# Depthwise tap sums that grow in SBUF instead of PSUM, and dummy products at the start, in a scan-convolution kernel on one Trainium2 core

## The chip, the cores and the metric

The kernel runs on one core of one Trainium2 chip. The metric is device time in microseconds of one execution, measured on the chip. A core has five engines that run their own instruction streams and meet only through semaphores: TensorE (PE: matrix products, output into PSUM), VectorE (DVE), ScalarE (ACT), GpSimd (POOL) and SyncE (SP, which here issues the transfers). SBUF is the working memory, 128 partitions wide; PSUM has eight banks of 512 float32 per partition. Everything here is float32.

## The reference

The input x is 4 images of 128 channels, 96 x 96. It is group-normalised, read out as four sequences of 9216 positions (rows forward, rows reversed, columns forward, columns reversed), and each sequence goes through the same block; the four results are fused and added to x.

```python
t = grouped1x1(x, in_proj_w, in_proj_b, 4)      # 128 -> 512 channels
u, gate = t[:, :256], t[:, 256:]
u = depthwise_conv(silu(u), dw_w)               # 5 taps along the sequence, 256 channels
s  = ssm_in_w @ u                               # 32 channels each
a  = DMIN + (DMAX - DMIN) * sigmoid(ssm_delta_w @ u + b)
bb = tanh(ssm_b_w @ u + b); cc = tanh(ssm_c_w @ u + b)
h  = scan(h = a * h + bb * s)                   # along the sequence
u  = u + ssm_out_w @ (cc * h + d * s)
u  = grouped1x1(u * sigmoid(gate), mix_w, mix_b, 4)
y  = out_proj_w @ u                             # back to 128 channels
out = x + fuse_w @ concat(the four y) + fuse_b
```

The depthwise convolution is the part that the change touches. It has five taps w[c, 0..4] for each of 256 channels: u[c, n] = sum over k of w[c, k] * silu(u)[c, n + k - 2].

## The kernel before

The work is cut into 384 units: 8 phases (4 images, two scan orders each), 6 steps in a phase, 4 residues p of the position modulo 4 in a step, and two sequences s = 0, 1 that run in opposite directions. The two units of one (phase, step, p) form a pair: there are 192 pairs, four to a step, 48 steps. `pair` emits the first six pairs, `pair_on` the others, `tail` what is left over. The order of each engine's instructions is the order in which these functions are written out; nothing reorders them, so an instruction that waits holds back everything behind it on its engine.

In the call of `pair_on` for pair t stand, in this order:

- products of the input projection for later steps, and ACT's SiLU of them into the tile `sil` (line 527);
- the convolution of pair t. Channels 0 to 127 go through PE: products with the diagonal matrices `band` and `less` into PSUM (line 130), completed either by DVE from the tile `lone` (line 691, in two pairs of each four) or by the `less` products and an ACT copy (lines 715, 717). Channels 128 to 255 go through the taps: ACT multiplies tap 0 (line 742, `first_tap`), and DVE adds taps 1 to 4, each as (source * weight) + partial sum (line 744). The four DVE instructions of a pair cover 128 partitions x 768 elements each (two sequences of 384 positions);
- DVE: half a step's scan in two pairs of each four (line 819), and at some places the statistics of the next image (line 445);
- POOL: c * h, plus d * s, and a copy (lines 825, 826, 828), five pairs behind the scan's input; the addition of the finished outputs of an older pair to the accumulator `acc` (line 879, two for a pair); later in the pair the decay and b * s for the scan (lines 792, 793);
- PE: the final product with the folded weights `w_fin` for the pair seven back, the state's contribution (line 577), gate products (line 557), and last the state projections of pair t (line 130, operand `main`), which read the finished `u` of pair t;
- ACT: copies of `u` into PSUM as a seed (line 589), outputs out of PSUM (lines 860, 862), tanh and copies (lines 593, 599, 781 to 802);
- DVE: the gating of the pair six back, one instruction for each sequence (line 638), which PE's next final products read. Behind it ACT emits tap 0 of pair t + 1.

The partial sum of the taps, `part`, lies in PSUM banks 0 and 1 (`TAPS = 0`). The same two banks hold the seed and the state's contribution of sequence 0 (`SSM = 0`), so the two uses of them take turns. Only the last tap writes `us[i][:, :, 1, :]`, the half of the tile `u` in SBUF that holds channels 128 to 255. `new_u` takes the tile `u` of a pair from a ring of eight.

`start` holds the first microseconds: loads of the first image with statistics on DVE, three filler products of 512 columns as soon as a chunk of x is there (line 1188), five smaller ones tied to the last statistics, the chain of small products and DVE instructions that gives the normalised weights, the folded weights, and the first pair.

Of the kernel before, what the change touches and what calls it, by code (L numbers as in the profile page):

```python
# [47 lines left out]
P = 128  # L48
B, DIM, HH, WW = 4, 128, 96, 96
L = HH * WW  # L50
HID, MH, K = 256, 32, 5
# [8 lines left out]
N = LN * WW // R  # L60
# [8 lines left out]
def conv_preact_kernel(  # L69
# [9 lines left out]
    nc = tc.nc  # L79
# [39 lines left out]


    psum = ps.tile([P, 8, 512], F32, name="psum")
    SSM, TAPS, PROJ = 0, 0, (4, 5)
    FRONT = (7, 6, 2, 3)

    def bank(i):
        return psum[:, i, :]
# [7 lines left out]
    gmeans = wp.tile([P, 2, P], F32, name="gmean")  # L134
# [32 lines left out]
    def stats_of(b):  # L167
        if b not in stats:
            stats[b] = sp.tile([P, NSC, 6], F32, tag="bn", name=f"bn_{b}")
        return stats[b]  # L170
# [127 lines left out]
    def fresh(step):  # L298

        return step * UB < NU and step % NS < NS // 2  # L300
# [75 lines left out]
    def less_rows(s, p):  # L376
        low = 64 * ((less_of(p) + s + 1) % 2)
        return slice(low, low + 64)
# [8 lines left out]
    for q in range(R):  # L387
        r = slice(32 * q, 32 * q + 32)
        nc.gpsimd.tensor_copy(id32[r, :], ident[r, r])
    for s in range(2):  # L390
        for p in range(R):
            for k in range(2):
                r, to = slice(0, P), band[:, s, p]
                if k == less_of(p):
                    r, to = less_rows(s, p), less[:, p]
                m = R * k - p + R - 1
                shape = [r.stop - r.start, 4, 32]
# [242 lines left out]
    us = {}  # L640

    def columns(step, sil, k):

        if fresh(step):
            return sil[..., k : k + N]
        return sil[..., 1 - k : 1 - k + N][..., ::-1]
# [80 lines left out]
    def new_u(i):  # L727
        us[i] = wk.tile([P, 2, 2, N], F32, tag="u", bufs=LAG + 2, name=f"u_{units[i]['id']}")

    def taps(i, ks, first=None):  # L730

        un = units[i]
        step = un["step"]
        sil = sils[step][:, :, 1] if fresh(step) else sils[step][:, ::-1, 1, ::-1]
        part = psum[:, TAPS : TAPS + 2, :N]
        for k in ks:
            off, q = divmod(un["p"] + k, R)
            src = columns(step, sil[:, :, q, :], off)
            if k == 0 and first:
                first.tensor_scalar_mul(part, src, w_tap[:, 0:1])  # L740
            elif k == 0:
                nc.scalar.activation(part, src, AF.Copy, scale=w_tap[:, 0:1])  # L742
            else:
                nc.vector.scalar_tensor_tensor(  # L744
                    us[i][:, :, 1, :] if k == K - 1 else part,
                    src,
                    w_tap[:, k : k + 1],
                    part,
                    ALU.mult,
                    ALU.add,  # L750
                )
# [51 lines left out]

    def first_tap(i):
        if i < NU:
            taps(i, range(1))

    def scan(step, part):
# [104 lines left out]
    def pair(t):  # L913
        i = 2 * t
        banks = head_banks(t)
        if t == R:
            load_lone(1)
        if t:
            new_u(i)
            taps(i, range(1, K))  # L920
            single = alone(units[i]["p"])
            conv(i, banks, single)
            if single:
                add_lone(i, banks)
            else:
                conv_less(i, banks, False)
                for s in range(2):
                    nc.vector.tensor_copy(us[i][:, s, 0, :], bank(min(banks) + s)[:, :N])
            first_tap(i + 2)
            front(t + R, FRONT if banks == PROJ else (5, 4, 2, 3))  # L930
        recurrence(t)
        stats_chunks(t)
        load_chunks(t + 2)
        proj(i, banks)
        n, s = divmod(t, 2)
        if s == 0:
            early[0] = tile_of(n) if n < 2 else shared()[:, : 4 * N].rearrange(
                "p (s j n) -> p s j n", s=2, j=2
            )
        for j in range(2):  # L940
            gate(2 * n, s, j, 2 + j)
        for j in range(2):
            tanh_one(n, early[0], s, j, 2 + j)
        load_gate(2 * n + s + UB)
        if n == 2 and s:
            nc.sync.dma_start(keep(n), early[0])
        for g in {0: (0, 1), 1: (2, 3)}.get(t, ()):
            keep_silu(0, g)
        if t > 3:
            nc.sync.dma_start(keep(t - 4), tile_of(t - 4))  # L950
        if t > 0:
            s = tbs[i - 2][0:64, :]
            nc.gpsimd.tensor_scalar(s, s, d_sb[0:64, 0:1], None, ALU.mult)

    def pair_on(t):
        i, k, n, end = 2 * t, t % R, t - LAG, NU // 2
# [28 lines left out]
            reload.clear()  # L985
        if t < end - 2:
            send()
        new_u(i)
        taps(i, range(1, K))
        conv(i, banks, single)  # L990
        if single:
# [194 lines left out]
    def start():  # L1186
        def filler(n):
            nc.tensor.matmul(  # L1188
                bank(7)[:, :n], accf[:, bass.ds(10 * SC, P)], accf[:, bass.ds(10 * SC, n)],
                start=True, stop=True,  # L1190
            )

        def outer(d, i, copy):
            for j in range(2):
                nc.tensor.matmul(  # L1195
                    bank(i)[:, bass.ts(j, P)], w_out[:, bass.ts(j, P)], w_fuse[:, d, :],
                    start=True, stop=True,
                )
            copy(w_of[:, d].rearrange("p j c -> p (j c)"), bank(i)[:, : 2 * P])

        def inner(ds, i):
            for n, (d, j) in enumerate((d, j) for d in ds for j in range(2)):
                nc.tensor.matmul(
                    bank(i)[:, bass.ts(n, P)], w_mix[:, j, :], w_of[:, d, j, :],
                    start=n == 0, stop=True, skip_group_check=True,
                )
            to = w_fin[:, ds[0] : ds[-1] + 1].rearrange("p d j c -> p (d j c)")
            nc.vector.tensor_scalar_mul(to, bank(i), 0.5)

        last_stats = stats_of(b0)  # L1210
        pieces = stats_first(b0)
        for n in (512, 512, 512):
            filler(n)
        next(pieces)
        for c, n in ((NSC - 5, 192), (NSC - 4, 192), (NSC - 3, 192), (NSC - 2, 192), (NSC - 1, 256)):
            nc.tensor.matmul(
                bank(7)[:, :6], accf[:, bass.ds(10 * SC, P)], last_stats[:, c, :], start=True, stop=True
            )
            filler(n)
        next(pieces)  # L1220
        outer(0, 0, nc.scalar.copy)
        outer(1, 1, nc.scalar.copy)
        next(pieces)
        outer(2, 4, nc.scalar.copy)
        next(pieces)
        outer(3, 5, nc.vector.tensor_copy)
        filler(128)
        for _ in pieces:
            pass
        sils[0] = new_sil(0)  # L1230
        banks = ((2, 3), (6, 7), (0, 1), (4, 5)), ((2, 3), (6, 7), (4, 5), (2, 3))

        def burst(j, g):
            for s in range(2):
                in_proj(0, g, s, j, banks[j][TURN.index(g) if j else g][s])

        def silus(j, g):
            for s in range(2):
                silu(0, g, s, j, banks[j][TURN.index(g) if j else g][s])
            edges(0, g, j, nc.vector)  # L1240

        def load_rows(j, r):
            for s in range(2):
                load_front(1, s, slice(64 * s + 32 * j, 64 * s + 32 * j + 32), r)

        for g in range(R):
            burst(0, g)
        silus(0, 0)
        burst(1, TURN[0])
        silus(0, 1)  # L1250
        burst(1, TURN[1])
        silus(0, 2)
        inner((0, 1), 0)
        inner((2, 3), 1)
        for w in (w_of, w_fuse):
            for e in (2, 1):
                nc.gpsimd.tensor_add(w[:, 0:e], w[:, 0:e], w[:, e : 2 * e])
        load_rows(0, slice(0, R))
        load_rows(1, slice(TURN[0], TURN[0] + 1))
        silus(0, 3)  # L1260
        new_u(0)
        burst(1, TURN[2])
        silus(1, TURN[0])
        taps(0, (0,), nc.vector)
        burst(1, TURN[3])
        load_rows(1, slice(TURN[1], R))
        load_rows(1, slice(0, TURN[0]))
        silus(1, TURN[1])
        taps(0, (1,))
        conv(0, head_banks(0))  # L1270
        silus(1, TURN[2])
        taps(0, (2,))
        silus(1, TURN[3])
        conv_less(0, head_banks(0))
        taps(0, (3, 4))
        keep_lone(0)
        load_lone(0)
        pf = bank(3)
        terms = [(w_of[:, 0, j, :], b_mix[:, j : j + 1]) for j in range(2)] + [(w_fuse[:, 0, :], b_out)]
        for i, (lhsT, rhs) in enumerate(terms):  # L1280
            nc.tensor.matmul(pf[:, 0:1], lhsT, rhs, start=(i == 0), stop=(i == len(terms) - 1))
        nc.scalar.activation(b_fin, pf[:, 0:1], AF.Identity, bias=b_fuse)
# [94 lines left out]
```

## Time and profile before

| | |
|---|---|
| median of 3 runs | 1738.51 us (1736.99 to 1743.14) |
| span of the profiled execution, first to last instruction | 1735.2 us |
| PE busy | 1713.6 us, 22522 instructions |
| DVE busy | 1507.9 us, 1508 instructions |
| ACT busy | 1494.8 us, 2544 instructions |
| POOL busy | 1447.0 us, 1490 instructions |
| granted TensorE clock | 1.000 |

The span is the time of the profiled execution between its first and its last instruction; no other time is given for that execution. It lies 3.3 us under the median of the runs. The rows of the profile give engine, line, operation, the tile written and the tiles read (out<-in), partitions x elements, and a count. "L744 ... psum<-sil,small,psum" is a tap that reads the source in `sil`, the weight in `small` and the partial sum in PSUM. A duration is from start to end as the profiler saw it; an instruction that has been dispatched and is held up inside its engine looks longer.

### The profile page before, as it was taken

How to read it: one execution, taken by the hardware profiler on the slowest of the kernel's cores; microseconds unless marked ns; L12 is line 12 of the kernel's file. 1: busy time of each engine (PE TensorE's matmuls, PEld its weight loads, DVE VectorE, ACT ScalarE, POOL GpSimd, SP SyncE). 2: the span in 40 equal slices, each digit the busy share in tenths (PEclk: the TensorE clock that was granted, in tenths of full speed). 3: DMA queues.
4: the chain of work that ended last, by engine and by line, in shares of the span. 5: the costliest groups of instructions: out<-in, count | busy, mean ns of one | idle time of the engine just before them, and what ended most of it. 6: DMA issues, size and time to landing. Idle time of an engine off the chain costs nothing.

```text
span 1735.2 us, 54226 instructions
## 1 busy us (share of the span) xinstructions
PE 1713.6 (99%) x22522; PEld 644.7 (37%) x22522; DVE 1507.9 (87%) x1508; ACT 1494.8 (86%) x2544; POOL 1447.0 (83%) x1490
## 2 busy tenths in 40 slices
PE   7999999999999999999999999999999999999998
PEld 4333333343333433344333443334333333333333
DVE  6899998888889998888889999888888888888887
ACT  4888988889888888888988888888998889888875
POOL 3689889888789988888788988887878889887887
PEclk9999999999999999999999999999999999999999
DMA  7746865358884786337896487433887548643364
GB/s 244 235 147 218 288 202 151 124 206 280 275 287 139 262 267 194 118 126 263 260 308 226 150 300 251 144 123 132 294 294 239 179 144 304 201 137 133 147 226 166
DMA packets 154644, 363.66 MB, mean 210 GB/s; under 512 B 19104, under 2 KB 120864, under 8 KB 154400
## 3 DMA queue, kind: packets, MB, share of 16 engines
q1 hardware_dynamic: 154256, 360.16, 62.8%
q8 instruction: 178, 2.92, 0.7%
q14 instruction: 66, 0.54, 0.1%
q10 hardware_dynamic: 144, 0.04, 0.0%
HBM read 221.41 MB, written 138.53 MB: 207 GB/s over the span
## 4 chain that ended last, share of the span: by engine, by line
PE 95%; DVE 2%; ACT 1%; DMA 1%; issue 0%; SPq 0%; DVEq 0%; ACTq 0%
PE psum L130 81%; PE psum L577 8%; PE psum L557 5%; DVE psum L744 1%; PE psum L1188 0%; DMA acc<-in_xr 0%; DMA kept<-shared 0%; DVE u L638 0%; ACT psum L589 0%; ACT psum L742 0%; DVE u L744 0%; ACT sil L527 0%; SPq L335 0%; PE psum L1195 0%; DVE u L691 0%
## 5 line engine op out<-in xcount | busy, mean ns | idle before, releaser
L744 DVE SCALAR_TENSOR_TENSOR psum<-sil,small,psum 128x768 f32<-128x768 f32 x576 | 589.1, 1023 | 42.2 <-ACT psum L742 16.8
L130 PE MATMUL psum<-u,w_fin 128*32 128x384 f32 (+1 forms) x6192 | 541.3, 484 | 1.1 <-ACT ys L860 0.4
L130 PE MATMUL psum<-u,main 128*32 128x384 f32 x6144 | 535.0, 489 | 0.5 <-DVE u L691 0.4
L638 DVE SCALAR_TENSOR_TENSOR u<-gate,psum 128x768 f32<-128x768 f32 x376 | 341.7, 950 | 150.0 <-PE psum L577 50.8
L879 POOL TENSOR_TENSOR acc<-ys,acc 128x384 f32<-128x384 f32 x375 | 411.8, 1120 | 14.0 <-ACT ys L860 1.9
L825 POOL TENSOR_TENSOR t<-t,t 64x384 f32<-64x384 f32 (+1 forms) x192 | 287.2, 1496 | 70.6 <-DVE t L819 48.3
L589 ACT COPY psum<-u 128x768 f32<-128x768 f32 x384 | 301.4, 799 | 10.5 <-DVE u L638 4.3
L130 PEld LDWEIGHTS psum<-u,w_fin 128*32 128x32 f32 x6192 | 195.2, 109 | 309.6 <-issue 235.5
L130 PEld LDWEIGHTS psum<-u,main 128*32 128x32 f32 x6144 | 180.0, 109 | 324.5 <-issue 218.3
L130 PE MATMUL psum<-sil,band 128*32 128x384 f32 x3072 | 285.3, 488 | 0.0
L792 POOL TENSOR_SCALAR t<-tm 64x384 f32<-64x384 f32 x184 | 170.8, 928 | 114.4 <-ACT tm L781 102.4
L826 POOL TENSOR_TENSOR t<-t,t 64x384 f32<-64x384 f32 (+1 forms) x192 | 233.9, 1218 | 15.1
L793 POOL TENSOR_TENSOR t<-t,tm 64x384 f32<-64x384 f32 x192 | 213.8, 1113 | 30.2 <-ACT t L784 15.5
L577 PE MATMUL psum<-t,main 32*128 32x384 f32 x1536 | 228.1, 525 | 4.2 <-ACT psum L589 4.2
L742 ACT ACTIVATE psum<-sil,small 128x768 f32<-128x768 f32 x191 | 172.6, 904 | 65.2 <-DVE u L638 61.9
L744 DVE SCALAR_TENSOR_TENSOR u<-sil,small,psum 128x768 f32<-128x768 f32 x192 | 194.9, 1015 | 6.8
L527 ACT ACTIVATE sil<-psum,bnorm 128x385 f32<-128x385 f32 x384 | 191.6, 584 | 4.0 <-DMA edge<-sil 0.9
L557 PE MATMUL psum<-x_in,wn 32*128 32x384 f32 x768 | 161.7, 498 | 0.0
L862 ACT COPY ys<-psum 128x384 f32<-128x384 f32 x288 | 132.3, 478 | 33.0 <-PE psum L130 28.3
L130 PEld LDWEIGHTS psum<-sil,band 128*32 128x32 f32 x3072 | 88.8, 108 | 171.4 <-issue 63.1
L781 ACT ACTIVATE tm<-psum,small 128x384 f32<-128x384 f32 x192 | 110.9, 578 | 14.0 <-PE psum L130 2.3
L577 PEld LDWEIGHTS psum<-t,main 32*128 32x128 f32 x1536 | 93.9, 183 | 73.7 <-issue 41.0
(108 smaller groups left out, 1512.3 us busy)
## 6 DMA issues: line engine op xcount, KB each, us to landing
gate<-kept SPq DMA_DIRECT2D x114, 768.0 KB, 5.2
kept<-gate SPq DMA_DIRECT2D x74, 768.0 KB, 3.7
sil<-sil SPq DMA_DIRECT2D x64, 770.0 KB, 6.6
lone<-edge SPq DMA_DIRECT2D x40, 770.0 KB, 7.5
x_in<-in_xs SPq DMA_DIRECT2D x250, 96.2 KB, 3.3
edge<-sil SPq DMA_DIRECT2D x96, 192.5 KB, 3.6
out<-acc SPq DMA_DIRECT2D x46, 384.0 KB, 6.4
acc<-in_xr SPq DMA_DIRECT2D x39, 384.0 KB, 6.4
```

The costliest lines, as they stand in the source:

```text
L130: nc.tensor.matmul(o[r, : rhs.shape[-1]], lhsT, rhs, start=start, stop=stop, skip_group_check=True)
L527: nc.scalar.activation(sils[step][:, s, j, g, :], bank(bk)[:, : N + 1], AF.Silu, bias=bn[:, 1:2] if j else bn[:, 4 + g : 5 + g],)
L557: nc.tensor.matmul(bank(to)[:, :N], stats[un["b"]][0][r, s, :], x_in[s][r, q, off : off + N], start=True, stop=True)
L577: nc.tensor.matmul(bank(ssm(bi, s) + j)[:, :N], w_so[r, bass.ts(j, P)], z[r, :], start=(bi, s) not in seeded, stop=True, skip_group_check= ...
L589: nc.scalar.copy(psum[:, ssm(bi, s) : ssm(bi, s) + 2, :N], us[bi][:, s])
L638: nc.vector.scalar_tensor_tensor(v, g, 1.0, pz, ALU.add, ALU.mult)
L742: nc.scalar.activation(part, src, AF.Copy, scale=w_tap[:, 0:1])
L744: nc.vector.scalar_tensor_tensor(us[i][:, :, 1, :] if k == K - 1 else part, src, w_tap[:, k : k + 1], part, ALU.mult, ALU.add,)
L793: nc.gpsimd.tensor_mul(ta[0:64, p, :], tb[0:64, :], tm[0:64, :])
L825: engine.tensor_mul(ta[0:64, p, r], tb[64:P, r], ta[64:P, p, r])
L826: engine.tensor_add(tb[0:64, r], ta[0:64, p, r], tb[0:64, r])
L879: adder.tensor_add(part, y, part)
```

## The change

There are two parts.

First, the partial sum of the taps is the `u` tile itself. Tap 0 (ACT) writes `us[i][:, :, 1, :]`, and taps 1 to 4 (DVE) read and write it in place. Nothing is left of the taps in PSUM banks 0 and 1, whose other use stays. `new_u` moves into `first_tap`, one pair earlier in the text, since tap 0 now needs the tile.

Second, `start` begins with 108 dummy products of the matrix `gmeans` with itself: tiles of 128 x 128, 128 x 32, 32 x 32, 32 x 128 and 64 x 32 with 256 or 192 columns, into banks 0 to 3. Nothing reads the results.

```diff
-    SSM, TAPS, PROJ = 0, 0, (4, 5)
+    SSM, PROJ = 0, (4, 5)
...
-        part = psum[:, TAPS : TAPS + 2, :N]
+        part = us[i][:, :, 1, :]
...
                 nc.scalar.activation(part, src, AF.Copy, scale=w_tap[:, 0:1])
             else:
                 nc.vector.scalar_tensor_tensor(
-                    us[i][:, :, 1, :] if k == K - 1 else part,
+                    part,
                     src,
                     w_tap[:, k : k + 1],
                     part,
...
     def first_tap(i):
         if i < NU:
+            new_u(i)
             taps(i, range(1))
...
         if t:
-            new_u(i)
             taps(i, range(1, K))
...
-        new_u(i)
         taps(i, range(1, K))
...
+        warm = gmeans.rearrange("p e c -> p (e c)")
+
+        def tiles(rows, cols, n=2 * P):
+            for r in range(0, P, rows):
+                for c in range(0, P, cols):
+                    nc.tensor.matmul(
+                        psum[c : c + cols, r // 32, :n], warm[r : r + rows, c : c + cols],
+                        warm[r : r + rows, :n], start=True, stop=True, skip_group_check=True,
+                    )
+
+        for shape in ((128, 128),) * 4 + (
+            (128, 32), (32, 32), (32, 32, 192), (32, 32, 192), (32, 128), (32, 32), (64, 32),
+            (32, 32), (128, 32), (128, 32),
+        ):
+            tiles(*shape)
         last_stats = stats_of(b0)
```

On DVE, two consecutive pairs in the first image, before. The scan's half comes from line 819, the gating from line 638, the taps from line 744; names of `u` are phase, step, p and s.

```order
L819 SCALAR_TENSOR_TENSOR t_2_1132<-t_2_1132,t_1_769 64x768
L638 SCALAR_TENSOR_TENSOR u_1_3_0_904<-gate_176,psum 128x768 x2
L744 SCALAR_TENSOR_TENSOR psum<-sil_747,small,psum 128x2x384 x3
L744 SCALAR_TENSOR_TENSOR u_3_2_0_1521<-sil_747,small,psum 128x2x384
L819 SCALAR_TENSOR_TENSOR t_2_1132<-t_2_1132 64x768
L638 SCALAR_TENSOR_TENSOR u_1_0_0_983<-gate_177,psum 128x768 x2
```

The same place after the change (the scan is at line 820 there):

```order
L820 SCALAR_TENSOR_TENSOR t_2_1241<-t_2_1241,t_1_878 64x768
L638 SCALAR_TENSOR_TENSOR u_1_3_0_932<-gate_176,psum 128x768 x2
L744 SCALAR_TENSOR_TENSOR u_3_2_0_1596<-sil_856,small,u_3_2_0_1596 128x2x384 x4
L820 SCALAR_TENSOR_TENSOR t_2_1241<-t_2_1241 64x768
L638 SCALAR_TENSOR_TENSOR u_1_0_0_1042<-gate_177,psum 128x768 x2
```

The instructions and their order are the same; all four taps now have both tensor inputs in SBUF (`sil` and `u`), where before each had one in SBUF and one in PSUM.

On ACT, around tap 0 in the same image, before, with the semaphores that each instruction waits for:

```order
L593 ACTIVATE gate_176<-psum,bnorm_272 128x384 [waits DMAHW5_49,PE_49]
L593 ACTIVATE gate_176<-psum,bnorm_272 128x384 [waits PE_49]
L742 ACTIVATE psum<-sil_747,small 128x2x384 [waits DVE_49]
L599 ACTIVATE gate_176<-psum,bnorm_272 128x2x384
L781 ACTIVATE tm_2_2_0_1241<-psum,small 128x384 [waits PE_49,Pool_49]
```

And after:

```order
L593 ACTIVATE gate_176<-psum,bnorm_380 128x384 [waits DMAHW5_49,PE_49]
L593 ACTIVATE gate_176<-psum,bnorm_380 128x384 [waits PE_49]
L742 ACTIVATE u_2_3_0_1327<-sil_856,small 128x2x384
L599 ACTIVATE gate_176<-psum,bnorm_380 128x2x384
L781 ACTIVATE tm_2_2_0_1350<-psum,small 128x384 [waits PE_49,Pool_49]
```

Tap 0 no longer waits for DVE's gating, which read banks 0 and 1; it stands at the same place.

On PE, the head of the program before:

```order
L1372 UNCONDITIONAL_BRANCH
L1188 MATMUL psum<-acc 128x512 x3
L1216 MATMUL psum<-bn_94,acc 128x6
L1188 MATMUL psum<-acc 128x192
L1216 MATMUL psum<-bn_94,acc 128x6
```

And after:

```order
L1386 UNCONDITIONAL_BRANCH
L1214 MATMUL psum<-gmean 128x256 x4
L1214 MATMUL psum<-gmean 32x256 x20
L1214 MATMUL psum<-gmean 32x192 x32
L1214 MATMUL psum<-gmean 128x256 x4
L1214 MATMUL psum<-gmean 32x256 x48
L1187 MATMUL psum<-acc 128x512 x3
L1230 MATMUL psum<-bn_94,acc 128x6
```

The 108 dummy products stand ahead of the fillers; behind them the order is the same.

## The prediction

> **What bounds the kernel now.** I read the page's busy times and its chain of waits first, then busy times by stretch, then DVE and POOL side by side in order of time, because the change gives DVE's most frequent instruction other operands.
>
> ```profile
> PE 1713.6 (99%) x22522; PEld 644.7 (37%) x22522; DVE 1507.9 (87%) x1508; ACT 1494.8 (86%) x2544; POOL 1447.0 (83%) x1490
> PE 95%; DVE 2%; ACT 1%; DMA 1%; issue 0%; SPq 0%; DVEq 0%; ACTq 0%
> ```
>
> PE is busy almost always and carries 95% of the chain that ended last. But DVE, ACT and POOL follow closely at 83 to 87%: whichever of them loses a sixth of its speed becomes the bound.
>
> ```profile
> 61.35:1709.35 1648.00, 1642.67 (x21552) 612.00 (x21545) 1447.52 (x1409) 1446.12 (x2457) 1405.78 (x1422) 1.00 0.63 209
> 549.00:583.75 34.75, 34.75 (x432) 13.89 (x416) 32.22 (x33) 30.60 (x51) 31.71 (x29) 1.00 0.48 151
> ```
>
> Columns: stretch, length, then busy us (count) of PE, weight loads, DVE, ACT and POOL, granted clock, DMA share, GB/s. From the first scan to the last lie 1648 us in 47.5 steps, 34.7 us each. The second row is one step, four pairs: DVE is busy for 32.2 of 34.75 us and POOL for 31.7. PE idles only 5.3 us in the whole first stretch, and this is the most that an easier life for any engine can return there.
>
> Now DVE in this part of the program (start, length, count at the end):
>
> ```profile
> 528.20 3.14 DVE L744 SCALAR_TENSOR_TENSOR psum<-sil,small,psum 128x768 f32<-128x768 f32 x3 [0.16 <-ACT psum L742]
> 531.37 1.01 DVE L744 SCALAR_TENSOR_TENSOR u<-sil,small,psum 128x768 f32<-128x768 f32 x1
> 532.30 1.01 DVE L691 SCALAR_TENSOR_TENSOR u<-lone,small,psum 128x768 f32<-128x768 f32 x1
> 533.23 1.01 DVE L445 BATCH_NORM_STATS2 bn<-xs 128x6 f32<-128x384 f32 x2
> 534.49 1.82 DVE L638 SCALAR_TENSOR_TENSOR u<-gate,psum 128x768 f32<-128x768 f32 x2 [0.25 <-PE psum L577]
> ...
> 549.00 3.08 DVE L819 TENSOR_TENSOR_SCAN t<-t,t 64x768 f32<-64x768 f32 x1
> ...
> 558.26 1.81 DVE L819 TENSOR_TENSOR_SCAN t<-t 64x768 f32<-64x768 f32 x1
> ```
>
> The first five rows are one pair with a `lone` instruction: four taps in 4.18 us, and 4.0 us for the rest up to the end of the gating. The last two are the same scan, once 3.08 and once 1.81 us. POOL at these times:
>
> ```profile
> 533.77 1.19 POOL L825 TENSOR_TENSOR t<-t,t 64x384 f32<-64x384 f32 x1
> ...
> 547.10 1.03 POOL L793 TENSOR_TENSOR t<-t,tm 64x384 f32<-64x384 f32 x1
> 548.08 2.39 POOL L879 TENSOR_TENSOR acc<-ys,acc 128x384 f32<-128x384 f32 x2
> 550.54 2.58 POOL L825 TENSOR_TENSOR t<-t,t 64x384 f32<-64x384 f32 x1
> ...
> 558.56 2.32 POOL L793 TENSOR_TENSOR t<-t,tm 64x384 f32<-64x384 f32 x1
> ```
>
> The scan dispatched at 549.00 met two additions that end at 550.47, and ended 1.61 us later, at 552.08: it stood still until POOL was done. POOL's next instruction began at 550.54 and ended at 553.12, 1.04 us after the scan, though it takes 1.19 alone. The scan at 558.26 came first, took its 1.81 us, and held up POOL's L793 for 2.32 us instead of 1.03; that ended 0.81 us after the scan. So one of the two stands still while the other works. The scan reads two tensors of SBUF, and so do these POOL instructions. It isn't special to the scan:
>
> ```profile
> 1713.56 0.88 DVE L825 TENSOR_TENSOR t<-t,t 64x384 f32<-64x384 f32 x1
> 1714.48 1.68 DVE L826 TENSOR_TENSOR t<-t,t 64x384 f32<-64x384 f32 x1
> ...
> 1713.79 1.74 POOL L825 TENSOR_TENSOR t<-t,t 64x384 f32<-64x384 f32 x1
> 1715.61 1.56 POOL L826 TENSOR_TENSOR t<-t,t 64x384 f32<-64x384 f32 x1
> ```
>
> In the tail both engines run ordinary products and sums of two SBUF tensors, and take strict turns: DVE to 1714.44, POOL to 1715.53, DVE to 1716.16, POOL to 1717.17. POOL got in during DVE's gap of 0.04 us. The taps as they are never stand still:
>
> ```profile
> L744 DVE SCALAR_TENSOR_TENSOR psum<-sil,small,psum x576: 1005/1023/1025, 31.5 to 1698.0; 128x768 f32<-128x768 f32 x192
> L819 DVE TENSOR_TENSOR_SCAN t<-t x56: 1752/2036/2636, 61.4 to 1709.3; 64x768 f32<-64x768 f32 x56
> L825 POOL TENSOR_TENSOR t<-t,t x192: 685/1224/2702, 70.2 to 1719.2; 64x384 f32<-64x384 f32 x190, 64x192 f32<-64x192 f32 x2
> L826 POOL TENSOR_TENSOR t<-t,t x192: 690/1221/2020, 71.5 to 1720.5; 64x384 f32<-64x384 f32 x190, 64x192 f32<-64x192 f32 x2
> L879 POOL TENSOR_TENSOR acc<-ys,acc x375: 987/1202/2541, 90.8 to 1727.5; 128x384 f32<-128x384 f32 x188
> L793 POOL TENSOR_TENSOR t<-t,tm x192: 1001/1015/2461, 39.3 to 1705.9; 64x384 f32<-64x384 f32 x192
> L792 POOL TENSOR_SCALAR t<-tm x184: 885/930/979, 38.4 to 1698.2; 64x384 f32<-64x384 f32 x184
> L828 POOL COPY t<-t 64x384 f32<-64x384 f32 x187 | 97.2, 520 | 11.9
> ```
>
> Shortest, median, longest in ns (the last row: busy us, mean): 576 taps with one input in PSUM lie between 1005 and 1025, whatever POOL does beside them. POOL's dependent instructions range over a factor of two or more.
>
> **The taps.** The change makes every tap an instruction with two SBUF inputs, of which there were none but the scan in the steady part. Number and order stay, and no transfer moves. Alone, a tap should cost what it does now: the fourth, which already writes SBUF, takes 1.01, and the gating, also SBUF to SBUF but for one input, 0.91 (half of 1.82); I take 1.02 and use the saving for the low end only.
>
> What a step demands of the shared way: DVE 16 taps x 1.02 + 2 scans x 1.81 = 19.9 us; POOL, by the medians, 4 x (2 x 1.20 + 1.22 + 1.22 + 1.02 + 0.93 + 0.52) = 29.3 us. Together 49.2, against a step of 34.75. A waiting instruction saves its start-up: the scan 1.81 - 1.61 = 0.20, POOL's 1.19 - 1.04 = 0.15 and 1.03 - 0.81 = 0.22, so 0.38 for a tap or scan and the POOL instruction behind it. With 18 such turns, 49.2 - 6.8 = 42.4 us.
>
> The two engines' own walks, with turns:
> - DVE. Tap 1 finds POOL halfway through an instruction (7.3 / 7 = 1.04 us on average): 0.52, then 1.02 - 0.20 = 0.82. Taps 2 to 4 each stand behind one POOL instruction: 0.04 + 0.86 + 0.82 = 1.72. Taps: 6.5 us. A `lone` pair adds 4.2 for the rest with its waits: 10.7. A scan pair adds 0.52 + 1.61 for the scan, 1.82 for the gating and some 0.45 of waits: 10.9. Step: 2 x 10.7 + 2 x 10.9 = 43.2 us.
> - POOL. 29.3 + 28 gaps of 0.07 (550.47 to 550.54) = 31.3. Each tap ahead of it adds 0.82 + 0.86 - 0.07 - 1.04 = 0.57, each scan 1.36: 16 x 0.57 + 2 x 1.36 = 11.8. Step: 43.1 us.
>
> Both come to 43 with neither ever short of work. In the step above DVE idled 2.5 us and POOL 3.0; 1.4 of DVE's is in its walk, so I add 1.0 and take 44.2. That is 9.45 us more than now, and x 47.5 steps = 449 us.
>
> The Trainium skill ("SBUF — State Buffer", section Who interferes with whom) says that a DVE instruction with two SBUF inputs and a POOL instruction that reads SBUF exclude each other, that whoever is first keeps the port for the whole instruction, and that the loser blocks fully. The exclusion agrees with the rows above, 3.08 against 1.81 us; "whole" does not quite, since the waiting side was done 0.15 to 0.22 us early. By that word a step would take 49.2 us, the rival B below.
>
> Who waits behind a tap that stands still: on DVE's queue the `lone` instruction, the scan and the gating; PE's projections need `u`, its next final products need the gating. PE has 8.7 us of work in a pair that will last 11, and ACT, fed by both, idles with it.
>
> **Tap 0 and the ring.** ACT's tap 0 loses a wait:
>
> ```profile
> ACT psum L742 <- DVE u L638: 61.9, 86, 1.7
> ```
>
> Those 61.9 us were spent off the path, under PE's products; their worth is bounded by PE's 5.3 us. With DVE as the bound, ACT waits for DVE elsewhere: zero. Taking the `u` tile earlier reuses that of the pair seven back, whose last readers, the final products, stand earlier on PE in the same pair; ACT has copied their results before tap 0. No wait arises. Free banks help nobody, since their other use keeps its place.
>
> **The dummy products.**
>
> ```profile
> 3.77 0.41 POOL L149 COPY gmean<-gmean 128x64 f32<-128x64 f32 x2
> 11.66 5.49 PE L1188 MATMUL psum<-acc 128*128 128x512 f32 x6 [11.66 <-DMA acc<-in_xr]
> 18.33 0.81 DVE L178 BATCH_NORM_AGGREGATE mv<-bn 128x2 f32<-128x144 f32 x1
> 19.69 0.68 PE L1188 MATMUL psum<-acc 128*128 128x256 f32 x2
> 20.30 0.24 PE L130 MATMUL psum<-mv,gmean 128*32 128x1 f32 x8
> 23.56 3.80 PE L130 MATMUL psum<-x_in,wn 32*32 32x385 f32 x96
> 30.72 1.50 PE L130 MATMUL psum<-sil,band 128*32 128x384 f32 x16
> 32.15 0.88 PE L130 MATMUL psum<-sil,less 64*32 64x384 f32 x16
> 37.64 1.05 PE L557 MATMUL psum<-x_in,wn 32*128 32x384 f32 x4
> ```
>
> PE was idle up to 11.66, and each product is two instructions. The dummies can begin at 4.2, when `gmeans` is complete. Scaled by columns from these rows: 80 of 32 x 32 some 3.9 us, 12 of 128 x 32 1.5, 8 of 64 x 32 0.6, 4 of 32 x 128 at most 1.4, 4 of 128 x 128 1.7 to 3.6 (a 512-column product took 1.83 at the beginning, a 256-column one at most 0.68 later, so PE begins slowly). That is about 9 us of work at full speed; with the first 5.5 us at half speed, as the fillers' 11.66 to 17.15 suggest, it ends near 16. The fillers behind it then run at full speed, 2.7 us instead of 5.5, and end near 18.5 instead of 17.15, so the first product of the statistics chain comes 1 us late. Bounds: 1.2 us earlier (statistics are done at 19.14, that product started at 20.30), 6 us later (all of it at half speed). I take +1.
>
> **Sum.** 1735.2 + 449 + 1 = 2185 for the profiled execution. The median of the runs stands 3.3 above the span: 2188, said as 2190. Less than 0.5% (8.7 us) can't be told from no change.
>
> **Rivals.**
>
> A, the forecast: turns, DVE and POOL as a joint bound, 2190. Low end: bare turns (42.4) with line 879 at its shortest, 0.99, in half the phases (8 x 0.21 / 2 = 0.85 less), so 41.6 a step: 1735 + 325 = 2060.
>
> B: no start-up saved, 49.2 a step: + 686, about 2425. For it: POOL's two additions kept the way together at 548.08. Against it: each turn quoted saves something.
>
> C: the taps' second SBUF input costs nothing, unlike the scan's, whose inputs lie on different partitions. Then PE stays the bound and the time is between 1729 and 1741: no change. It decides whether a tap beside a POOL instruction stays at 1.02 us. Against it: the tail's two DVE instructions, of which the second took 1.68 beside 0.88.
>
> D: PE's clock falls because PE now idles. Idle time per pair would be 11.05 - 8.7 = 2.4 us, in one or two pieces. Were PE at half speed throughout, a step would take 69.5 us and the kernel 3390. Against it: the granted clock is 1.00 in every row above. The Trainium skill ("TensorE: Matmul & The Clock Gate", Part 1: The HAM clock gate) gives about 3.4 us of idleness before the rate halves; no run here shows that yet.
>
> E: POOL and DVE miss each other more than I assume, 1745 to 2060: half of the taps meet no POOL instruction.
>
> **How the numbers follow.** A 0.86, B 0.06, C 0.04, D 0.02, E 0.02. The time is A's. The range goes from A's low end, 2060, to B, 2425, and leaves out C, D and E. Slower: A, B, D and E, 0.96; within 0.5%: most of C, 0.035; faster: 0.005.
>
> **What would show it.** Taps with a mean of 1.5 to 1.9 us and a minimum near 1.0; means of lines 825, 826, 879 and 793 up by some 0.5 us; scans longer on average; PE's work unchanged near 1715 us but 78% of the span; DVE and POOL above 90%; the chain of waits led by DVE line 744 and POOL; the first product of the statistics chain near 21 us. Taps at 1.02 with an unchanged span would make me wrong by C, a granted clock under 0.95 by D, a step under 41 us by too many turns assumed.

## The result and the profile after

The changed kernel takes 2103.47 us in the median (2101.51 to 2108.28), against 1737.75 us before on the same chip: a ratio of 1.2104, 95% interval 1.2082 to 1.2126. The span of the profiled execution is 2101.3 us, 366 more than the 1735.2 of before.

The page's busy times and chain of waits, after:

```profile
PE 1872.2 (89%) x22738; PEld 658.9 (31%) x22738; DVE 1919.1 (91%) x1508; ACT 1495.6 (71%) x2544; POOL 1907.5 (91%) x1490
PE 33%; POOL 27%; DVE 25%; issue 10%; ACT 5%; DMA 0%; POOLq 0%; DVEq 0%; SPq 0%; ACTq 0%
```

DVE and POOL are now the busiest, at 91% each. DVE gained 411 us of busy time and POOL 460, with the same number of instructions; ACT's work did not change. The chain, 95% of which was PE, now runs through PE, POOL and DVE in parts of 33, 27 and 25%. Busy time by stretch, from the first scan to the last (columns as in the prediction):

```profile
65.09:2075.24 2010.15, 1791.98 (x21564) 622.33 (x21559) 1857.88 (x1409) 1447.78 (x2459) 1863.52 (x1423) 0.96 0.52 172
```

47.5 steps in 2010.15 us are 42.3 us each, against 34.7. That stretch holds 362 of the 366 us; the first scan comes 3.7 us later than before, and the tail is as long as it was. The taps, by source line (shortest, median, longest in ns), and POOL's groups (busy us, mean ns, idle before):

```profile
L744 DVE SCALAR_TENSOR_TENSOR u<-sil,small,u x768: 1004/1641/4009, 32.0 to 2060.3; 128x768 f32<-128x768 f32 x192
```

```profile
L744 DVE SCALAR_TENSOR_TENSOR u<-sil,small,u 128x768 f32<-128x768 f32 x768 | 1197.0, 1559 | 93.4 <-ACT u L742 71.9 <-ACT sil L527 0.8
L880 POOL TENSOR_TENSOR acc<-ys,acc 128x384 f32<-128x384 f32 x375 | 595.1, 1608 | 12.5 <-ACT ys L861 1.9
L827 POOL TENSOR_TENSOR t<-t,t 64x384 f32<-64x384 f32 x190 | 293.5, 1545 | 14.9
L792 POOL TENSOR_SCALAR t<-tm 64x384 f32<-64x384 f32 x184 | 260.7, 1417 | 37.8 <-ACT tm L781 22.4
L829 POOL COPY t<-t 64x384 f32<-64x384 f32 x187 | 200.3, 1071 | 11.9
```

The shortest tap still takes 1.00 us; the median tap takes 1.64 and the longest 4.01. Before, all lay between 1005 and 1025 ns. All of DVE's gain is theirs: 1197.0 us against 784.0. On POOL the addition (line 880, before 879) went from a mean of 1120 to 1608 ns, line 792 from 928 to 1417, the copy from 520 to 1071. How the two alternate is seen in order of time, one stretch of DVE and then of POOL:

```profile
673.04 1.81 DVE L820 TENSOR_TENSOR_SCAN t<-t 64x768 f32<-64x768 f32 x1
674.89 1.82 DVE L638 SCALAR_TENSOR_TENSOR u<-gate,psum 128x768 f32<-128x768 f32 x2
676.62 6.54 DVE L744 SCALAR_TENSOR_TENSOR u<-sil,small,u 128x768 f32<-128x768 f32 x4
683.08 1.00 DVE L691 SCALAR_TENSOR_TENSOR u<-lone,small,psum 128x768 f32<-128x768 f32 x1
684.01 1.01 DVE L445 BATCH_NORM_STATS2 bn<-xs 128x6 f32<-128x384 f32 x2
684.94 1.87 DVE L638 SCALAR_TENSOR_TENSOR u<-gate,psum 128x768 f32<-128x768 f32 x2
```

```profile
676.23 1.22 POOL L827 TENSOR_TENSOR t<-t,t 64x384 f32<-64x384 f32 x1
677.51 1.12 POOL L829 COPY t<-t 64x384 f32<-64x384 f32 x1
678.71 3.62 POOL L880 TENSOR_TENSOR acc<-ys,acc 128x384 f32<-128x384 f32 x2
682.42 1.48 POOL L792 TENSOR_SCALAR t<-tm 64x384 f32<-64x384 f32 x1
683.98 1.00 POOL L793 TENSOR_TENSOR t<-t,tm 64x384 f32<-64x384 f32 x1
685.06 1.19 POOL L826 TENSOR_TENSOR t<-t,t 64x384 f32<-64x384 f32 x1
```

Four taps take 6.54 us, and in that time POOL passes the copy and the two additions in 1.12 and 3.62 us; before, the copy's mean was 0.52 and an addition's median 1.2. As soon as DVE is at instructions with one SBUF input (683.08 to 686.81), POOL's run at their own length: 1.00 and 1.19 us.

### The profile page after: what moved, and what is told of

Its sections match the earlier page's. It is cut to its first block, busy times and chain, and to the rows that moved or that the text cites. A ratio compares the mean times of both kernels' runs of the same rounds, so it can differ in the third digit from the quotient of the medians.

```text
span 2101.3 us, 54779 instructions
## 1 busy us (share of the span) xinstructions
PE 1872.2 (89%) x22738; PEld 658.9 (31%) x22738; DVE 1919.1 (91%) x1508; ACT 1495.6 (71%) x2544; POOL 1907.5 (91%) x1490
## 4 chain that ended last, share of the span: by engine, by line
PE 33%; POOL 27%; DVE 25%; issue 10%; ACT 5%; DMA 0%; POOLq 0%; DVEq 0%; SPq 0%; ACTq 0%
PE psum L130 26%; DVE u L744 14%; POOL acc L880 8%; DVE t L820 5%; POOL t L792 4%; POOL t L793 4%; POOL t L827 4%; DVE u L638 3%; POOL t L826 3%; PE psum L557 3%; PE psum L577 3%; POOL t L829 3%; DVE u L691 2%; ACT sil L527 1%; ACT u L742 1%
## 5 line engine op out<-in xcount | busy, mean ns | idle before, releaser
L744 DVE SCALAR_TENSOR_TENSOR u<-sil,small,u 128x768 f32<-128x768 f32 x768 | 1197.0, 1559 | 93.4 <-ACT u L742 71.9
L130 PE MATMUL psum<-u,main 128*32 128x384 f32 x6144 | 574.8, 515 | 74.1 <-DVE u L691 40.1
L880 POOL TENSOR_TENSOR acc<-ys,acc 128x384 f32<-128x384 f32 x375 | 595.1, 1608 | 12.5 <-ACT ys L861 1.9
L826 POOL TENSOR_TENSOR t<-t,t 64x384 f32<-64x384 f32 (+1 forms) x192 | 267.3, 1392 | 69.1 <-DVE t L820 56.2
L589 ACT COPY psum<-u 128x768 f32<-128x768 f32 x384 | 301.7, 800 | 17.9 <-DVE u L638 14.9
L827 POOL TENSOR_TENSOR t<-t,t 64x384 f32<-64x384 f32 (+1 forms) x192 | 296.2, 1543 | 15.1
L792 POOL TENSOR_SCALAR t<-tm 64x384 f32<-64x384 f32 x184 | 260.7, 1417 | 37.8 <-ACT tm L781 22.4
L577 PE MATMUL psum<-t,main 32*128 32x384 f32 x1536 | 267.8, 537 | 10.3 <-ACT psum L589 7.2
L793 POOL TENSOR_TENSOR t<-t,tm 64x384 f32<-64x384 f32 x192 | 226.0, 1177 | 15.0
L802 ACT ACTIVATE t<-t,small 64x384 f32<-64x384 f32 x186 | 113.9, 616 | 152.7 <-POOL t L793 102.6
L829 POOL COPY t<-t 64x384 f32<-64x384 f32 x187 | 200.3, 1071 | 11.9
L742 ACT ACTIVATE u<-sil,small 128x768 f32<-128x768 f32 x191 | 176.9, 926 | 0.0
L593 ACT ACTIVATE gate<-psum,bnorm 128x384 f32<-128x384 f32 x152 | 88.1, 582 | 108.2 <-PE psum L557 90.0
```

The source lines that it names most:

```text
L130: nc.tensor.matmul(o[r, : rhs.shape[-1]], lhsT, rhs, start=start, stop=stop, skip_group_check=True)
L577: nc.tensor.matmul(bank(ssm(bi, s) + j)[:, :N], w_so[r, bass.ts(j, P)], z[r, :], start=(bi, s) not in seeded, stop=True, skip_group_check= ...
L589: nc.scalar.copy(psum[:, ssm(bi, s) : ssm(bi, s) + 2, :N], us[bi][:, s])
L744: nc.vector.scalar_tensor_tensor(part, src, w_tap[:, k : k + 1], part, ALU.mult, ALU.add,)
L792: nc.gpsimd.tensor_scalar(*decay(i))
L793: nc.gpsimd.tensor_mul(ta[0:64, p, :], tb[0:64, :], tm[0:64, :])
```

## The experiments

The theory after the result: taps with two SBUF inputs and POOL instructions that read SBUF exclude each other, and DVE and POOL, taking turns, set the pace. Its rivals: the taps are slow by themselves in SBUF; the dummy products carry a part; PE's clock, which fell to 0.961, carries a part.

### One part of the change alone

The first kernel is the one before with the dummy products:

```diff
+        warm = gmeans.rearrange("p e c -> p (e c)")
...
+        for shape in ((128, 128),) * 4 + (... the ten other shapes ...):
+            tiles(*shape)
         last_stats = stats_of(b0)
```

> The kernel before with the 108 dummy products alone; the taps stay in PSUM. Turn-taking theory (all of the loss comes from taps that take turns with POOL): within 2 us of the kernel before, the first product of the statistics chain at 20.4 us as in the changed kernel against 20.30 before. Rival (the dummies themselves move the time, by the PE clock or by a later start): 5 us or more either way.

Measured: 1738.85 us in the median of 11 runs against 1737.10 of 15, ratio 1.0013 (1.0004 to 1.0022). PE's first instructions:

```profile
4.23 9.90 PE L1215 MATMUL psum<-gmean 128*128 128x256 f32 x216 [4.23 <-POOL gmean L149]
14.07 2.84 PE L1188 MATMUL psum<-acc 128*128 128x512 f32 x6
...
20.20 0.24 PE L130 MATMUL psum<-mv,gmean 128*32 128x1 f32 x8
...
24.94 3.66 PE L130 MATMUL psum<-x_in,wn 32*32 32x385 f32 x88 [0.64 <-DMA x_in<-in_xs]
```

The dummies fill idle time up to 14.1 us, the fillers behind them run at twice the speed (2.84 us for three instead of 5.49), and the statistics chain begins at 20.20, 0.1 us earlier than before. In this execution PE then waited for a transfer of `x_in`, and the first pair came 1.2 us later; whether that is what the 1.75 us of the median consist of was not tried. The dummies cost a little (0.7 to 3.8 us by the interval) and gain nothing.

The second kernel is the changed one without the dummy products (the lines above taken out).

> The changed kernel without the dummy products. Turn-taking theory: 2100 to 2107 us, as the changed kernel, taps at a mean of 1.55 us. Rival (the dummies carry part of the loss): under 2095 us.

Measured: 2100.15 us, ratio 1.2091 (1.2075 to 1.2108), taps at a mean of 1562 ns. Without the dummies 363 of the 366 us remain: the loss comes from the taps that grow in `u`, with tap 0 and the ring tile, which belong to that part of the change.

### A dose of one and of two taps

Tap 0 writes `u`; the first one or two DVE taps read it there, the others grow in PSUM. The dummy products stay in.

```diff
-                    part,
+                    part if DOSE <= k < K - 1 else grown,
                     src,
                     w_tap[:, k : k + 1],
-                    part,
+                    part if k > DOSE else grown,
```

Here `part` is PSUM banks 0 and 1 again, `grown` the half of `u`, and DOSE is 1 or 2.

> Tap 0 is written to u, the first DVE tap reads it there (two SBUF inputs) and writes PSUM; taps 2 to 4 as before, so one DVE tap of four has two SBUF inputs. Turn-taking theory: this tap waits about half a POOL instruction, 0.35 us a pair, 1.4 us a step, and DVE had 2.5 us of idle time in a step, so most of it is hidden: 1738 to 1800 us; the first tap of a pair has a mean near 1.4 us and the three others stay at 1.02 us. Rival (a tap in SBUF costs in proportion, because of the tap itself): a quarter of the loss, about 1830 us.

> As the kernel with one tap, but the first two DVE taps have two SBUF inputs. Turn-taking theory: the second tap lets one POOL instruction in ahead of it, 0.70 us more a pair; a step of DVE is 32.2 + 4 x 1.05 = 36.4 us and some idle time, so 1800 to 1900 us: more than proportional to the kernel with one tap. Rival (in proportion): half of the loss, about 1920 us.

Measured: one tap 1773.6 us, ratio 1.0211 (1.0197 to 1.0225); two taps 1872.55 us, 1.0792 (1.0775 to 1.0808). With four it is 1.2104. The first tap in SBUF costs 37 us, the second 99, the third and fourth together 231. The taps of the kernel with one:

```profile
L746 DVE SCALAR_TENSOR_TENSOR psum<-sil,small,psum x384: 1021/1023/1024, 35.4 to 1733.4; 128x768 f32<-128x768 f32 x192
...
L746 DVE SCALAR_TENSOR_TENSOR psum<-sil,small,u x192: 1018/1194/1972, 34.0 to 1731.3; 128x768 f32<-128x768 f32 x192
L746 DVE SCALAR_TENSOR_TENSOR u<-sil,small,psum x192: 1015/1015/1016, 37.5 to 1734.5; 128x768 f32<-128x768 f32 x192
```

Only the tap with two SBUF inputs is stretched (mean 1309 ns, near 1400 forecast); those with an input in PSUM stay at 1.02 us, also the one that writes SBUF. So it is the second read from SBUF, not the write. PE still carries 78% of that kernel's chain: most of the first dose is hidden under PE, as the forecast of both ranges assumed, and a loss in proportion (1830 and 1920 us) is refuted.

### POOL's side

The additions into the accumulator are left out, in the changed kernel and in the one before:

```diff
-                adder.tensor_add(part, y, part)
+                if adder is not nc.gpsimd:
+                    adder.tensor_add(part, y, part)
```

> The changed kernel without POOL's additions into the accumulator (line 880), so the output lacks the computed part. POOL's demand falls from 29.3 to 19.7 us a step. Turn-taking theory: two POOL instructions fewer to take turns with in a pair, a step of about 37 to 40 us, 1840 to 1980 us, taps at a mean of 1.25 to 1.45 us. Rival (taps in SBUF are slow by themselves, by their in-place chain or by SBUF): unchanged near 2103 us and 1.56 us a tap.

> The control: the kernel before without the same additions, with the same part of the output missing. Both theories: PE stays the bound, 1725 to 1740 us, taps at 1.02 us.

Measured: 1822.45 us, ratio 1.0484 (1.0462 to 1.0506) to the full kernel before; the control took 1743.83 us in one run. Taps in the first kernel:

```profile
L744 DVE SCALAR_TENSOR_TENSOR u<-sil,small,u x768: 1002/1343/2008, 31.3 to 1778.4; 128x768 f32<-128x768 f32 x192
```

The taps were not touched, and yet their median fell from 1641 to 1343 ns and 281 of the 366 us are gone, more than I expected (1840 to 1980). The control is 4 us above my range for it. Its excess lies in the start, where the granted clock was 0.50 from 26.3 to 39.95 us and the first scan came at 69.1 us, not 61.4; from the first scan to the last it took 1647.5 us, as the kernel before with 1648.0. So the additions themselves bound nothing before. A tap that is slow by itself is refuted.

Then each addition becomes three memsets, which write SBUF and read nothing:

```diff
+                    for _ in range(3):
+                        adder.memset(ys, 0.0)
```

> The changed kernel in which each POOL addition (line 880) is replaced by three memsets of ys, some 0.4 us each: POOL stays as busy but these instructions only write SBUF; the output lacks the computed part. If only POOL instructions that read SBUF take turns with the taps: as without the additions, 1840 to 1980 us. Rival (any busy POOL holds the taps up, or POOL's own load is the bound): near 2103 us.

Measured: 1918.74 us in one run. The memsets, and the taps beside them:

```profile
L882 POOL MEMSET ys<- x1125: 408/418/428, 95.3 to 1910.2; 128x384 f32 x188
```

```profile
L744 DVE SCALAR_TENSOR_TENSOR u<-sil,small,u x768: 1003/1141/2055, 31.6 to 1875.5; 128x768 f32<-128x768 f32 x192
```

1125 memsets among 768 taps, and none took longer than 428 ns: a POOL instruction that only writes is not held up. POOL is as busy as in the changed kernel (91%), but the taps' median is 1141 ns, not 1641. It is 96 us slower than without the additions. My reading is that POOL's load counts too, but as load: the memsets take 2.4 us of POOL's time in a pair while its other instructions still take turns, and POOL carries 45% of this kernel's chain. No run tried that apart.

### The PE clock

In the changed kernel the granted clock fell to half in 38 short stretches, each 3.41 or 6.83 us long, one or two windows of 3.41 us. A mean of 0.961 over 2101.3 us means 164 us at half speed. PE was busy for 149 us of them, so it lost some 75 us of work, and at most 82. One of the stretches, by windows of 3.41 us:

```profile
422.86:426.27 3.41, 3.39 (x34) 1.09 (x27) 3.34 (x3) 3.33 (x7) 3.27 (x3) 1.00 0.33 91
426.27:429.68 3.41, 2.57 (x15) 0.89 (x14) 3.38 (x4) 0.76 (x2) 3.33 (x3) 1.00 0.00 0
429.68:433.09 3.41, 3.41 (x28) 1.06 (x28) 2.66 (x4) 2.55 (x4) 3.17 (x4) 0.50 0.07 26
433.09:436.50 3.41, 3.41 (x48) 1.29 (x44) 3.34 (x3) 2.39 (x5) 3.27 (x3) 1.00 0.87 296
```

PE idled for 0.84 us of the second window, and in the third its clock was 0.50; the projections (32 instructions) took 4.38 us there instead of 2.79. To see what this is worth, PE got more work where it idles:

```diff
+        for _ in range(2):
+            gate_of(1, 0, 7)
+            gate_of(0, 0, 6)
         gate_of(0, 1, 5)
...
+        if gated is None:
+            for bk in PROJ:
+                nc.tensor.matmul(bank(bk)[:, : 2 * P], gmean, gmeans.rearrange("p e c -> p (e c)"),
+                                 start=True, stop=True, skip_group_check=True)
         proj(i, PROJ, not fronted)
```

> The changed kernel with more work for PE where it idles: four repeated gate products in pairs that have them, two products of gmean before the state projections in the others, some 1.5 us a pair. Theory that turn-taking alone sets the time: the granted clock rises to 0.99 or more, and the time stays within 1% of 2103 us, since DVE and POOL are the bound. Rival (the PE clock that falls at half speed for 164 us carries a good part of the loss): 2050 us or less, by up to 82 us of PE time that comes back.

Measured: 2141.21 us, 1.2322 (1.2301 to 1.2343): 38 us slower than the changed kernel, with the clock at 0.980. Both expectations missed. PE was busy for 2006.0 us, 94%, and the extra products also came ahead of gate products and projections that others wait for: DVE's wait for tap 0 grew from 71.9 to 155.3 us. This run does not tell what the clock costs. The next asks it the other way round and takes PE work away, as much as the clock takes:

```diff
-                mm(bank(b0 + s), g, less[r, p, g, :], columns(step, sil[s][r, g, :], k),
-                   False, True)
+                if i < 2 * LAG:
+                    mm(bank(b0 + s), g, less[r, p, g, :], columns(step, sil[s][r, g, :], k),
+                       False, True)
...
-        conv(i, banks, single)
+        conv(i, banks, True)
```

The last two lines make the `band` products end the sum in PSUM, which the `less` products did.

> The changed kernel without the `less` products (line 130, operands sil and less) from the seventh pair on, so a part of one tap of channels 0 to 127 is missing in the output. They are some 80 us of PE time, as much as the lowered clock takes from PE (164 us at half speed). DVE, POOL and their turns are untouched. If DVE and POOL alone set the pace: 2095 to 2106 us. If PE's time counts by its share of the chain that ended last (33%): about 2075 us. If PE's lost time counts in full: about 2020 us.

Measured: 2100.2 us, 1.2087 (1.2067 to 1.2107), at a clock of 0.959. Its busy times:

```profile
PE 1828.1 (87%) x21266; PEld 665.1 (32%) x21266; DVE 1921.3 (91%) x1508; ACT 1483.0 (71%) x2544; POOL 1906.4 (91%) x1490
```

PE has 44 us less to do by this row (the products themselves filled 84 us before), and the time is 3 us lower, which lies within the intervals of the two ratios. So PE's work, spread evenly, is worth next to nothing here. PE's 33% of the chain is not a share of what a faster PE would bring: in this run PE's part fell to 25%, POOL's and DVE's rose to 30 and 27%, and the time hardly moved.

The lowered clock comes in lumps, right behind PE's waits, so it is a question of its own. The changed kernel's trace answers it in part. Steps at the same place in different images do the same work, and some have a stretch at half speed where others have none. From the first DVE tap of a step's third pair to that of the next step, in two places, each once without and once with such a stretch (columns as in the prediction):

```profile
591.29:633.18 41.89, 36.96 (x456) 13.12 (x460) 41.34 (x33) 33.34 (x56) 38.59 (x28) 1.00 0.60 197
1107.16:1149.07 41.91, 38.53 (x456) 13.58 (x460) 41.36 (x33) 33.50 (x56) 38.61 (x28) 0.96 0.60 198
...
1279.57:1323.52 43.95, 36.80 (x512) 12.60 (x504) 43.40 (x36) 31.06 (x56) 39.39 (x33) 1.00 0.56 168
248.72:292.61 43.89, 37.71 (x496) 12.80 (x500) 42.98 (x37) 29.88 (x54) 39.34 (x33) 0.96 0.58 174
```

PE is busy for 0.9 to 1.6 us more at the lowered clock, and the steps are equally long to 0.06 us. A third step at the second place, also with 3.4 us at half speed, took 44.28 us. Where the places can be compared, then, the lowered clock costs 0.0 to 0.4 us a step; most places have no step without it, so its price over the whole kernel stays an inference.

## Why the prediction was right, and where it was off

- The mechanism held in each part: only instructions with two SBUF inputs are stretched, only POOL instructions that read are held up, and the bound moved from PE to DVE and POOL together. Rivals C (no exclusion) and B (nothing saved, 2425 us) fell. The shortest taps, at 1.00 us, show that growing in SBUF costs nothing alone.
- The size was 86 us too high: 44.2 us a step were forecast, 42.3 measured. By DVE's walk: the taps were sized at 6.5 us a pair, 26.0 a step, and took 16 x 1.56 = 24.9. By the trace 71 of the 768 took at most 1.03 us and met no wait, a small part of rival E. The step that I walked holds statistics (line 445) in both `lone` pairs, 2.0 us; over the 48 steps they average 36.4 / 48 = 0.8. There one busy step had been taken for the mean. Against that the scans were too cheap: 4.2 forecast, (126.0 + 104.0) / 48 = 4.8 measured. The waits were taken as 2.4, and DVE's idle time is (2010.15 - 1857.88) / 47.5 = 3.2. These four terms, partly against each other, make 0.9 of the 1.9 us; the rest was not traced to a term.
- For POOL I named four lines that would grow by some 0.5 us each. Only the addition (line 880) did, by 0.49. The sum (line 827, before 826) grew by 0.33, line 793 hardly (1113 to 1177), and the product of c and h got shorter (1504 to 1400): by the trace it overlapped a scan 43 times before and 25 times after. Line 792 and the copy, which I had not named, grew by 0.49 and 0.55; line 792 had shown no stretch before (885 to 979 ns).
- I expected the chain of waits to be led by DVE's line 744 and POOL. PE still has the largest part, 33%, and line 744 has 14%.
- PE's busy time was forecast unchanged near 1715 us and 78%; it is 1872 and 89%. The dummies are 8 us of it (PE is busy for 1721.8 us in the kernel with them alone) and the lowered clock some 75; the remaining 75 or so were not traced to a cause.
- Rival D, the clock: I gave it one or two pieces of 2.4 us of idle time in a pair and kept the clock at 1.00. By PE's waits (in total, times, longest) the longest piece was 4.3 us, where a gate product waits for a bank that DVE's `lone` instruction still has to read:

```profile
PE psum L557 <- DVE u L691: 68.1, 28, 4.3
```

  And the clock fell after much shorter pieces, 0.82 us in the stretch shown above. D happened in small, 0.961 in the mean, and its price was next to nothing where it could be read.
- The dummies were put at +1 us; alone they cost 1.75 (0.7 to 3.8). The path was another than forecast: the statistics chain was not late (20.43, not 21), since the dummies ended at 14.9 and not near 16.
- Tap 0's lost wait and the earlier ring tile were put at zero. Neither was tried apart. Tap 0 now holds DVE up more than before: the taps' idle time until ACT had written it rose from 16.8 to 71.9 us in all, 1.5 us a step, which is part of the waits above.

## What to carry to other kernels

Before a partial sum is moved from PSUM to SBUF, count the inputs that each DVE instruction then reads from SBUF: with two of them it took turns here with the POOL instructions that read SBUF, and both engines paid. What this costs depends not only on the instruction's own length but on the sum of both engines' demand in a period, less what either does meanwhile without the other; here it cost 37 us for one tap in four, 366 for all. An existing instruction of that kind (here the scan, 1.8 to 3.9 us long) shows the price in the profile before the change is made.

## What the runs showed of the hardware that was not expected

- The PE clock fell to half after windows of 3.41 us in which PE had idled far less than the whole window: 0.84 us in the stretch shown. The 38 stretches begin on one grid of such windows. Of the windows before which the clock was full, those with 2 us of idle time or more were followed by a fall in 20 cases of 21, those with 0.8 to 2 us in 15 of 96, those with less in 3 of 355. What else decides is open.
- POOL's memsets of 128 x 384 took only 408 to 428 ns beside taps with two SBUF inputs, while the sum of line 827 took 1.60 us in the mean on POOL in the same kernel, against 1.22 before.
- An engine that is busy for 89% of the span and carries the largest part of the chain was not the bound: some 80 us of work taken from PE moved the time by 3 us.
